# A written-out order of a cross-attention kernel's operations is replaced by another one

## The chip, the cores and the metric

The kernel runs on one core of a Trainium2 chip. The core has five instruction streams that run side by side and wait for one another by semaphores: TensorE (PE, matrix products and transposes; its weight loads are shown apart as PEld), VectorE (DVE), ScalarE (ACT), GpSimd (POOL) and SyncE (SP, which here only issues transfers between the memory of the device and that of the core). The metric is the time of one execution on the device in microseconds (us); less is better. A change below 0.3% (1.7 us here) can't be told from none.

## The reference

All arrays are 32-bit floats. `x` is 2 x 2048 x 640, the context 2 x 128 x 384; there are 8 heads of 80 numbers. Shortened to what is computed (B = 2 batches, H = 640):

```python
enc, ca = ctx[:, :124], ctx[:, 124:]              # 124 tokens of text, 4 extra ones
query, keyt, valt = x @ Wq, enc @ Wk, enc @ Wv
hs = mha(query, keyt, valt)                        # 8 heads, softmax over 124 keys
ca_q1 = einsum("btc,th->bch", ca, Wq_ca)[:, indices]   # 384 rows, spread over 2048 by linspace
ca_hs1 = mha(ca_q1, x, x)                          # softmax over 2048 rows of x
ca_hs2 = mha(ca_hs1 @ Wq, ca @ Wk_ca, ca @ Wv_ca)  # softmax over 4 keys
out = (hs + ca_hs2) @ Wout + b_out + x
```

## The kernel before

**Staging.** The work falls into stretches, each taken batch by batch. The rows of `x` come in blocks of 512 (`x_load`: pieces `xi` by transfer, turned by DVE into `xt`); PE makes the queries (`pq`) of each block, and of each block a few small products (`pyz`, `yz`) that ACT, DVE and POOL make into operands `zop`, `cop` and `y_sb` of the extra attention. The function `adapter(b)` does the extra attention of one batch. Its first half multiplies `zop` and `cop` into score tiles `s` of four PSUM banks each ("quads", 24 a batch); DVE reduces each quad to its maxima (`mx`). There is room for one quad: `quad` is `Room(1)`, and the step of DVE that reads a quad frees it. Its second half makes 24 more quads a batch, of which ACT makes exponentials (`ea`) and PE sums (`acc`). At a batch's end the sums go through ACT (`accs`), a transpose on PE (`pt_acc`) and then through `second(b)`: DVE divides (`r`, `prod`), reduces (`s2f`, `m`, `p`), ACT takes an exponential of `p`, DVE sums and turns it (`r`, `p2t`), and PE multiplies it with `rows` into `pt_p`, whose result goes out by a transfer and comes back as part of the probabilities of the text attention.

The text attention works on 16 units of 256 rows (`text(m)`): scores `sc` from the keys (`kmain`, `krest`) and the queries (`text_scores`), a softmax on DVE, ACT and DVE or POOL (`m`, `p`, `r`, the multiplication `p<-p,r`), a transposition `eb` on DVE with a round trip through the device's memory (`kept`, `pT`), the hidden rows `ph`, and the output products `po` with the parts of `Wout`. In seven units (`BY_SUMS`) the products are made with fewer rows by sums of operands (`text_out_fast`: `wout_sums`, `hs`); in the others with a high part, a low part and a mixed part of `Wout` and of the hidden rows (`text_out`: `wout_top`, `wout_low`, `wout_mix`, `ks`). DVE adds each `po` to the rows of `x` with the bias (`x_more`, `last_rows`), and SP stores the rows (`stored`). The parts `wout_low` and `wout_mix` are made after the last `acc` of batch 1, in the room of `y_sb`.

**What sets the order.** Each function is a task: a generator that yields steps `Do(engine, fn, after, needs, frees, marks, grows)`. `after` names what must have been issued before, `needs` takes places in rooms, `frees` gives them back, `marks` makes names known. The class `Desk` holds a table `ORDER` of 2366 entries; an entry is a task's number, with a letter where the engine is chosen (`a` ACT, `v` DVE, `g` POOL, `n` none). `Desk.run` walks the table, and every entry issues the next step of its task:

```python
for entry in self.ORDER.split():
    task = self.tasks[int(entry.rstrip("avgn"))]
    op = task.op
    self.engine = self.SIDES.get(entry[-1], op.engines[0])
```

Each instruction is pinned to that place, so the table sets the order of each engine's stream, of SP's transfers too. All engines run their streams in order; nothing moves at run time. L221 and L229 are the helpers of all products and transposes, L225 that of the warming products `unread`, L236 that of all work on DVE, ACT and POOL, L246 that of all transfers.

Of the kernel before, what the change touches and what calls it, by code (L numbers as in the profile page):

```python
# [8 lines left out]
F32 = mybir.dt.float32  # L9
# [5 lines left out]
P = 128  # L15
# [52 lines left out]
class Desk:  # L68
# [7 lines left out]
    2 4 4 0 2 36 0 0 2 0 0 2 0 0 2 0 0 2 0 0 2 2 124 2 4 2 0 128a 0 2 0 6 6 6 2 125 4 6 130a 126 4 131a 127 4 4  # L76
    132a 6 133v 2 3 4 6 3a 2 15 3 6 3a 15 15 3 6 3v 3 7 7 8 8 7 8 11 7 7 15 0 8 135a 0 134a 7 5 8 7 7 15 9 7
    137a 6 1 138a 136v 14 8 12 15 7 7 7 139a 7 7 141v 140v 7 142a 9 15 143a 8 144 15 9 8 8 36 8 145 5 15 15 8 8
    9 10 8 9 5 146 5 9 147 15 14 36 15 15 148 6 9 9 9 14 14 14 14 9 14 9 14g 129 152a 151v 149a 12 150v 15 153 6
    6 9 36 14 129 15 14 36 16 14g 11 9 129 129 101 36 155 155 12 155 155 11a 36 157 11 9 12 9 156a 9 155 12 158  # L80
    158 159v 158 158 158 9 36 160 162v 18 12 36 163a 12 13 36 117 123 158 17 154 158 158 158 154 154 39 161 123
    17 117v 161 165g 154 161 117v 171 175 17 161 166g 161 164 18 164 164 17 18 117g 36 164 117g 154 154 164 117g
    164 161 18 176a 164 36 164g 161 16 36 18 18 167g 171 177 16 164 16 16 16 18 36 178a 117v 117 18 43 16 36 16g
    171 181 161 117g 18 18 180 164 168g 180 36 182a 16 17 180 117g 179 180 36 179 16 171 183 16g 174 185 184a 18
    180 18 180 18 36 172 186 36 174 18 17 17 179 18 179 174 188 170 187 187 19 20 21 161 21 187 187 172 192 187
    20 189 190 21 187 36 43 36 179 179 21 173 203 203 203 191 191 36 193 191 173 204 169 103 203 191 180 36 180g
    203 191 19 21 203 21 194g 180 36 19 200 209 20 21 195g 19 36 19 191 21 39 102 210a 191 19 21 21 36 19 191
# [162 lines left out]
def kernel(  # L250
# [2116 lines left out]
```

## Time and profile before

| | us |
|---|---|
| time, median of 3 runs (lowest to highest) | 564.38 (563.48 to 564.88) |
| span of the profiled execution, first to last instruction | 562.1 |
| PE busy | 549.2 (98%) |
| DVE busy | 402.2 (72%) |
| ACT busy | 276.3 (49%) |
| POOL busy | 208.1 (37%) |
| mean granted clock of TensorE | 0.997 |

A time of the profiled execution by the clock of the runs is not recorded; the three times lie 1.4 to 2.8 us above its span, the median 2.3. The busy times are means over the whole span. In the stretch of the first quads of batch 0 (45.9 to 158.9 us) DVE is busy 105.16 of 113.0 us, in that of batch 1 (251.5 to 343.6 us) 87.97 of 92.1.

### The profile page before, as it was taken

What the parts mean: (1) busy time and instruction counts of PE and PEld (TensorE: products, weight loads), DVE (VectorE), ACT (ScalarE), POOL (GpSimd) and SP (SyncE); (2) the same over time, 40 slices, a digit from 0 to 9 for tenths busy, and PEclk for the clock granted to TensorE, in tenths of its full rate; (3) what the DMA queues carried; (4) which work ended last, traced back from release to release, by engine and by line L of the source; (5) the groups of instructions that cost most, each with busy time, mean ns of one, the idle gap of its engine ahead of it and who ended that gap; (6) DMA issues with size and microseconds to landing.
All of it is one profiled execution on the core that took longest, in us unless ns stands there. A gap on an engine that the chain in (4) does not pass through costs nothing.

```text
span 562.1 us, 17332 instructions
## 1 busy us (share of the span) xinstructions
PE 549.2 (98%) x7338; PEld 337.8 (60%) x7338; DVE 402.2 (72%) x621; ACT 276.3 (49%) x752; POOL 208.1 (37%) x206
## 2 busy tenths in 40 slices
PE   9999999999999999999999999999999899999997
PEld 8563455556555655455365445455554477989796
DVE  2457999999996564589999998655735886449542
ACT  3122645445338898886524524589878432111200
POOL 7002625344424522013559364512424830441040
PEclk9999999999999999999999999999999989999999
DMA  8994759774876899446558895859865367977533
GB/s 258 244 175 121 163 123 166 163 159 142 170 199 155 183 251 180 136 160 176 177 126 247 226 232 133 255 149 254 244 172 177 74 124 215 264 215 195 160 123 129
DMA packets 151549, 101.38 MB, mean 180 GB/s; under 512 B 86476, under 2 KB 130012, under 8 KB 151472
## 3 DMA queue, kind: packets, MB, share of 16 engines
q1 hardware_dynamic: 150704, 99.88, 69.5%
q8 instruction: 58, 0.95, 0.8%
q0 software_dynamic: 768, 0.40, 0.4%
q14 instruction: 19, 0.16, 0.1%
HBM read 61.34 MB, written 38.90 MB: 178 GB/s over the span
## 4 chain that ended last, share of the span: by engine, by line
PE 82%; DVE 7%; DMA 5%; ACT 2%; issue 2%; SPq 1%; DVEq 0%; ACTq 0%
PE po L221 23%; PE pq L221 23%; PE acc L221 7%; PE sc L221 6%; PE s L221 6%; PE ph L221 5%; PE pq_first L221 3%; PE pyz L221 3%; DVE mx L236 2%; ACT p L236 1%; DMA bias<-in_L_xattn_b_out_dram 1%; PE pk L221 1%; PE unread L225 1%; ACT ea L236 1%; PE pv L221 1%
## 5 line engine op out<-in xcount | busy, mean ns | idle before, releaser
L236 DVE TENSOR_REDUCE mx<-s 128x4 f32<-128x2048 f32 x48 | 109.2, 2275 | 2.9 <-PE s L221 2.8
L236 POOL TENSOR_TENSOR p<-p,r 128x992 f32<-128x992 f32 x29 | 53.8, 1856 | 141.1 <-DVE r L236 135.0
L236 ACT ACTIVATE ea<-s 128x2048 f32<-128x2048 f32 x48 | 90.4, 1884 | 25.6 <-PE s L221 25.3
L236 ACT ACTIVATE p<-sc,m 128x124 f32<-128x124 f32 x256 | 89.5, 374 | 25.7 <-DVE m L236 25.7
L236 ACT ACTIVATION_READ_ACCUMULATOR p<-sc,m 128x1 f32 x256 | 55.5, 217 | 0.0
L221 PE MATMUL pq<-xt,wq_sb 128*32 128x256 f32 x896 | 54.3, 381 | 0.6 <-DVE q L236 0.6
L236 DVE TENSOR_REDUCE m<-sc 128x4 f32<-128x496 f32 x64 | 40.6, 662 | 13.9 <-PE sc L221 13.7
L221 PE MATMUL acc<-ea,y_sb 128*32 128x384 f32 (+2 forms) x768 | 50.1, 383 | 0.0
L221 PE MATMUL ph<-pT,vpad 128*32 128x256 f32 x768 | 45.8, 380 | 0.8 <-DMA out_dram<-x_more 0.3
L236 DVE STREAM_TRANSPOSE eb<-p 128x1024 f32<-128x1024 f32 x32 | 39.5, 1233 | 4.5 <-POOL p L236 3.3
L221 PEld LDWEIGHTS pq<-xt,wq_sb 128*32 128x32 f32 x896 | 27.5, 110 | 22.9 <-issue 5.5
L221 PEld LDWEIGHTS sc<-kmain,q 64*128 64x128 f32 x512 | 31.8, 187 | 11.6 <-issue 8.4
L221 PE MATMUL pq<-xt,wq 128*32 128x512 f32 x320 | 38.8, 595 | 0.0
L221 PE MATMUL po<-wout_sums,hs 128*32 128x320 f32 x448 | 35.4, 438 | 3.5 <-DVE x_more L236 2.9
L221 PE MATMUL sc<-kmain,q 64*128 64x124 f32 x512 | 37.5, 283 | 0.1
L221 PE MATMUL po<-wout_sb,hs 128*32 128x320 f32 (+1 forms) x452 | 36.4, 434 | 0.7 <-DVE prod L236 0.6
L221 PE MATMUL po<-wout_low,ks 128*128 128x320 f32 x204 | 35.7, 308 | 0.0
L221 PEld LDWEIGHTS ph<-pT,vpad 128*32 128x32 f32 x768 | 24.4, 110 | 18.6 <-issue 2.6
L236 POOL TENSOR_TENSOR last_rows<-last_rows,bias 128x640 f32<-128x640 f32 x10 | 17.0, 1697 | 44.7 <-DMA last_rows<-in_x_dram 44.7
L221 PE MATMUL po<-wout_top,ks 128*128 128x320 f32 x180 | 32.5, 311 | 0.0
L221 PEld LDWEIGHTS acc<-ea,y_sb 128*32 128x32 f32 x768 | 21.1, 109 | 17.3 <-issue 8.6
L221 PEld LDWEIGHTS po<-wout_low,ks 128*128 128x128 f32 x204 | 31.3, 188 | 0.0
(232 smaller groups left out, 951.4 us busy)
## 6 DMA issues: line engine op xcount, KB each, us to landing
kept<-eb SPq DMA_DIRECT2D x32, 512.0 KB
pT<-kept SPq DMA_DIRECT2D x48, 256.0 KB
landing<-away SPq DMA_DIRECT2D x60, 128.0 KB
xi<-in_x_dram SPq DMA_DIRECT2D x28, 256.0 KB
x_more<-in_x_dram SPq DMA_DIRECT2D x17, 320.0 KB
out_dram<-x_more SPq DMA_DIRECT2D x16, 320.0 KB
last_rows<-in_x_dram SPq DMA_DIRECT2D x15, 320.0 KB
out_dram<-last_rows SPq DMA_DIRECT2D x14, 320.0 KB
```

The source lines that it names most:

```text
L221: self.pin(self.nc.tensor.matmul(out[strip], lhsT[:, strip], rhs, **kw))
L225: self.pin(self.nc.tensor.matmul(out, zeros, zeros, start=True, stop=True))
L236: return lambda *args, **kw: self.pin(getattr(engine, what)(*args, **kw))
```

## The change

The table `ORDER` is another one, of the same tasks and steps; a first and a last line of it show that it can only be read by what it does to the streams. The engine letters of some steps differ too: eight multiplications `p<-p,r` are on DVE instead of three, and eighteen additions of the bias instead of eleven. The rest of the change is small: rooms grow and come free through the steps' own lists (`grows`, `frees`) instead of inside functions, the step of the mixed part of the hidden rows is split off as `raw` and `mixing`, and a store is a task of its own in `text(m)` that waits by name for the additions to its rows instead of being started by the last of them.

```diff
     ORDER = """
-    2 4 4 0 2 36 0 0 2 0 0 2 0 0 2 0 0 2 0 0 2 2 124 2 4 2 0 128a 0 2 0 6 6 6 2 125 4 6 130a 126 4 131a 127 4 4
...
+    132 618 120 634 641 635 635 89 641 132 637 637 639 130 639 131 636 88 636 90
     """
...
-                op = yield Do("PE", scores, [("cop", b)], needs=[(quad, 1), (eas, 1)])
+                st = pieces(v)[-1][0]
+                ends_ = j == 1 and 512 * (v + 1) == CAD * (st + 1) and st % 4 == 3
+                op = yield Do(
+                    "PE", scores, [("cop", b)], needs=[(quad, 1), (eas, 1)],
+                    frees=(lambda st=st: [(zops, room_of["zop", b, st // 4])]) if ends_ else (),
+                )
...
             op = yield Do(
                 "PE", product, [("q", n), "keys", ("rest", m, k)], needs=[(banks, 2), (es, 1)], marks=[("sc", m, k)],
-            )
-            rests.give(rest_of[m, k][1])
+                frees=lambda k=k: [(rests, rest_of[m, k][1])],
+            )
...
-                op = yield Do("DVE", add, [op.at], frees=[(banks, s)] if end else [])
+                op = yield Do(
+                    "DVE", add, [op.at], frees=[(banks, s)] if end else [], marks=[("added", m, i, n, k)],
+                )
                 at = [op.at]
-                key = (m, i, 2)
-                ends.setdefault(key, []).append(op.at)
-                if len(ends[key]) == 4:
-                    yield Fork(stored(*key, ends[key]))
...
+            if m in BY_SUMS:
+                parts = (((0, 0), (0, 2), (2, 0), (3, 0)), ((0, 1), (0, 3), (1, 0), (1, 1)))[k]
+                added = [("added", m, k, *part) for part in parts]
+            else:
+                added = [("added", m, k, v) for v in ((0, 1) if u == 2 else (u,))]
+            yield Do(
+                "SP", store, added,
+                frees=lambda: [(rows, xr_of[m][k][1])] if u == 2 else [],
+            )
```

What this makes of the streams is shown at three places. In the changed kernel the helpers' lines are five smaller (L216, L224, L220, L231, L241).

The first is SP's stream near the start, where it loads the weights `w_kca`, `w_k`, `w_vca` and `w_v` and the nine pieces `xi_1` of the second block of `x`. Before:

```order
L246 DMA w_kca<-in_L_xattn_Wk_ca_dram 128x3x640
L246 DMA w_k<-in_L_xattn_Wk_dram 128x3x640
L246 DMA xi_1_268<-in_x_dram 32x64x32
L246 DMA xi_1_268<-in_x_dram 32x16x16 x2
L246 DMA w_vca<-in_L_xattn_Wv_ca_dram 128x3x640
L246 DMA xi_1_268<-in_x_dram 32x64x32
L246 DMA xi_1_268<-in_x_dram 32x16x32
L246 DMA w_v<-in_L_xattn_Wv_dram 128x3x640
```

After:

```order
L241 DMA w_kca<-in_L_xattn_Wk_ca_dram 128x3x640
L241 DMA xi_1_260<-in_x_dram 32x64x32
L241 DMA xi_1_260<-in_x_dram 32x16x16 x2
L241 DMA xi_1_260<-in_x_dram 32x64x32
L241 DMA xi_1_260<-in_x_dram 32x16x32
L241 DMA xi_1_260<-in_x_dram 32x64x32
L241 DMA xi_1_260<-in_x_dram 32x16x32
L241 DMA xi_1_260<-in_x_dram 32x64x32
L241 DMA xi_1_260<-in_x_dram 32x16x32
L241 DMA w_k<-in_L_xattn_Wk_dram 128x3x640
L241 DMA w_vca<-in_L_xattn_Wv_ca_dram 128x3x640
L241 DMA w_v<-in_L_xattn_Wv_dram 128x3x640
```

All nine pieces now stand ahead of `w_k`; before, `w_k` stood ahead of them and four more followed `w_v`. On DVE the copies `k<-w_k` now stand behind the five transpositions of these pieces and ahead of the copy `a<-pa` that feeds PE's transposes `pt_a`; before, `k<-w_k` and `a<-pa` stood ahead of those transpositions.

The second place is DVE's stream between the third and the fourth quad of batch 0. Before:

```order
L236 TENSOR_REDUCE mx_461<-s_0_0_1_0_683 128x4
L236 STREAM_TRANSPOSE yt_0_0_727<-yz_0_509 128x512
L236 STREAM_TRANSPOSE yt_0_1_732<-yz_0_509 128x512
L236 TENSOR_TENSOR wq_sums<-wq_sb 128x256 x2
L236 TENSOR_REDUCE m_0_0_752<-sc_0_0_734 128x4
L236 TENSOR_REDUCE m_0_1_753<-sc_0_1_735 128x4
L236 TENSOR_REDUCE mx_461<-s_0_0_1_1_719 128x4
```

After:

```order
L231 TENSOR_REDUCE mx_506<-s_0_0_1_0_718 128x4
L231 TENSOR_TENSOR wq_sums<-wq_sb 128x256
L231 TENSOR_REDUCE m_0_0_753<-sc_0_0_735 128x4
L231 STREAM_TRANSPOSE yt_0_0_784<-yz_0_539 128x512
L231 STREAM_TRANSPOSE yt_0_1_790<-yz_0_539 128x512
L231 STREAM_TRANSPOSE xt_2_730<-xi_2_415 128x512
L231 TENSOR_REDUCE m_0_1_754<-sc_0_1_736 128x4
L231 COPY q_757<-pq_0_758 128x2x256
L231 STREAM_TRANSPOSE xt_2_730<-xi_2_415 128x512
L231 TENSOR_REDUCE mx_506<-s_0_0_1_1_797 128x4
```

The transpositions of the third block of `x` and a copy of queries have come in between.

The third place is the end of batch 1's extra attention. On DVE before, from the last two `wout_low` to `p2t`; two more `wout_low`, `prod` and `r<-pt_acc` stand right ahead of the first row:

```order
L236 TENSOR_TENSOR wout_low<-wout_sb,wout_top_5690 128x640
L236 TENSOR_TENSOR wout_low<-wout_sb,wout_top_5692 128x640
L236 TENSOR_TENSOR wout_mix_5827<-wout_top_5694,wout_low 128x640
L236 TENSOR_TENSOR wout_mix_5828<-wout_top_5735,wout_low 128x640
L236 TENSOR_REDUCE s2f<-prod 128x8x3 x3
L236 TENSOR_REDUCE m_1_5837<-s2f 128x24
L236 TENSOR_TENSOR p_1_5732<-s2f,m_1_5837 128x96
L236 TENSOR_TENSOR x_more<-x_more,po_1_5840 128x320
L236 TENSOR_TENSOR wout_mix_5826<-wout_top_5692,wout_low 128x640
L236 TENSOR_REDUCE r_1_5734<-p_1_5732 128x24
L236 RECIPROCAL r_1_5734<-r_1_5734 128x24
L236 TENSOR_TENSOR p2t_5733<-p_1_5732,r_1_5734 128x3x8x4
```

After, from the second `wout_low` to `p2t`; another `wout_low` and two `wout_top` stand right ahead of the first row:

```order
L231 TENSOR_TENSOR wout_low<-wout_sb,wout_top_5743 128x640
L231 RECIPROCAL r_1_1_5796<-pt_acc_1_5792 128x12
L231 TENSOR_TENSOR prod<-pt_acc_1_5792,r_1_1_5796 128x3x96
L231 TENSOR_TENSOR wout_low<-wout_sb,wout_top_5759 128x640
L231 TENSOR_TENSOR wout_low<-wout_sb,wout_top_5758 128x640
L231 TENSOR_REDUCE s2f<-prod 128x8x3 x3
L231 TENSOR_REDUCE m_1_5841<-s2f 128x24
L231 TENSOR_TENSOR p_1_5736<-s2f,m_1_5841 128x96
L231 TENSOR_TENSOR last_rows<-last_rows,po_0_5718 128x320
L231 TENSOR_REDUCE r_1_5738<-p_1_5736 128x24
L231 RECIPROCAL r_1_5738<-r_1_5738 128x24
L231 TENSOR_TENSOR p2t_5737<-p_1_5736,r_1_5738 128x3x8x4
```

Two `wout_low` have moved ahead of `r<-pt_acc`, and the three `wout_mix` have moved behind `p2t`. On PE at the same place before, from the product that follows the scores of unit 15 to `pt_p`; `pt_acc` and those scores (eight products with `kmain`, eight with `krest`) stand ahead:

```order
L221 MATMUL po_1_5840<-wout_sums,hs_4309 32x320 x8
L221 MATMUL ph_0_5865<-pT_4532,vpad_107 32x256 x8
L221 MATMUL po_2_5879<-wout_sb,hs_4309 32x320 x8
L221 MATMUL po_2_5879<-wout_sb,wout_sums 32x320 x4
L221 MATMUL ph_2_5892<-pT_4532,vpad_107 32x256 x8
L221 MATMUL po_0_5703<-wout_sums,hs_4309 32x320 x8
L221 MATMUL ph_4_5915<-pT_4532,vpad_107 32x256 x8
L221 MATMUL po_1_5840<-wout_sums,hs_4309 32x320 x8
L221 MATMUL po_1_5840<-wout_sb,wout_sums 32x320 x4
L221 MATMUL pt_p_1_5950<-rows_5772,p2t_5733 32x512
```

After, from `pt_acc` on, with the scores of unit 15 ahead of it:

```order
L224 MATMUL pt_acc_1_5792<-ident,accs_1_5762 128x128 x3
L216 MATMUL po_0_5718<-wout_sums,hs_4318 128x320 x2
L216 MATMUL ph_0_5826<-pT_5370,vpad_107 32x256 x8
L216 MATMUL po_1_5856<-wout_sums,hs_4318 32x320 x8
L216 MATMUL ph_2_5865<-pT_5370,vpad_107 32x256 x8
L216 MATMUL po_3_5875<-wout_sb,hs_4318 32x320 x8
L216 MATMUL po_3_5875<-wout_sb,wout_sums 32x320 x4
L216 MATMUL po_0_5718<-wout_sums,hs_4318 32x320 x8
L216 MATMUL pt_p_1_5899<-rows_5757,p2t_5737 32x512
```

The scores of unit 15 have moved ahead of `pt_acc`, and fewer products stand between it and `pt_p`.

Elsewhere, the fourteen products `unread` all stand at the head of PE's stream (before: nine, three behind the first `pt_x`, two later), and after `pt_acc` of the first half of batch 1's sums PE has a quad and eight strips of `acc` before the first `po` (before: one `po` of three products and a quad). The table's entries between 240 and 350 us of the profile before have nearly the same order in both.

More of the change, by code (lines that the diff above doesn't have):

```diff
@@ L1587, in adapter @@
                 if j == 1 and 512 * (v + 1) == CAD * (st + 1) and st % 4 == 3:
-                    zops.give(room_of["zop", b, st // 4])
+                    late["ps_"]=0
         yield Fork(second(b))
@@ L1711, in more @@
                 late["ps"] = ctx.enter_context(tc.tile_pool(name="ps_r", bufs=1, space=bass.MemoryType.PSUM))
-                banks.grow(4)
-            yield Do("NONE", more, [])
+            yield Do("NONE", more, [], grows=[(banks, 4)])
         def product(s):
@@ L2225, in text_out, with raw, mixing, first @@
         )
+    def raw(t):
+        return t.bitcast(F32)
+    def mixing(mix, top, low, after, marks):
+        def first():
+            if desk.engine == "ACT":
+                desk.a_activation(mix(), raw(low()), AF.Identity, scale=UP)
+            else:
+                mixed(mix(), raw(top()), raw(low()))
+        op = yield Do(("DVE", "ACT"), first, after)
+        def second():
+            if op.ran == "ACT":
+                minus(mix(), raw(top()), raw(mix()))
+        yield Do(("NONE", "POOL", "DVE"), second, marks=marks)
     def hidden_parts(m, c0, n, hs, ph, s, at):
@@ L2237, in hidden_parts @@
         )
-        def scaled():
-            if desk.engine == "ACT":
-                desk.a_activation(cols("mix"), cols("low", True), AF.Identity, scale=UP)
-            else:
-                mixed(cols("mix"), cols("top", True), cols("low", True))
-        op = yield Do(("DVE", "ACT"), scaled)
-        both = op.ran == "ACT"
-        yield Do(
-            ADDS if both else "NONE", lambda: both and minus(cols("mix"), cols("top", True), cols("mix", True)),
-            marks=[("hs mix", m, c0)],
-        )
+        yield from mixing(lambda: cols("mix"), lambda: cols("top"), lambda: cols("low"), [("hs low", m, c0)], [("hs mix", m, c0)])
     def out_part(m, i, u, hs):
@@ L2275, in add, with stored, store @@
             desk.v_scalar_tensor_tensor(t, po[:, :HALF], 1.0 + DOWN, t, ALU.mult, ALU.add)
[L2277 to L2283 removed]
+        yield Do("DVE", add, [op.at, ("xr", m, i)], frees=[(banks, s)], marks=[("added", m, i, u)])
     spans = (0, HALF), (HALF, H), (0, H)
[L2286 removed]
+    def stored(m, k):
         b, st = tiles(m)[k]
[L2289 to L2294 removed]
+        for u in (2,) if m < UNITS - 1 else (0, 1):
+            def store(u=u):
+                cols = slice(*spans[u])
+                dma(out[b, st * P : (st + 1) * P, cols], xr_of[m][k][0][:, cols])
+            if m in BY_SUMS:
+                parts = (((0, 0), (0, 2), (2, 0), (3, 0)), ((0, 1), (0, 3), (1, 0), (1, 1)))[k]
+                added = [("added", m, k, *part) for part in parts]
+            else:
+                added = [("added", m, k, v) for v in ((0, 1) if u == 2 else (u,))]
[3 more added lines that the diff above has]
+            )
     blocks = [(b, sb) for b in range(B) for sb in range(NSB)]
@@ L2304, in text @@
         yield Fork(probabilities(m))
+        for k in range(2):
+            yield Fork(stored(m, k))
     begin = desk.begin
```

183 lines of the change are left out of this document (80 added, 103 removed).

## The prediction

> **What bounds the kernel now.** I read the page first, then PE's waits, then the stretches, then the timeline at each place where PE waited.
>
> ```profile
> span 562.1 us, 17332 instructions
> PE 549.2 (98%) x7338; PEld 337.8 (60%) x7338; DVE 402.2 (72%) x621; ACT 276.3 (49%) x752; POOL 208.1 (37%) x206
> ```
>
> PE is busy 549.2 of 562.1 us, and both orders give it the same products. A new order can win no more than PE's 12.9 idle microseconds and what a lower clock costs, but it can lose any amount. PE's waits say where most of it is:
>
> ```profile
> PE po L221 <- DVE x_more L236: 2.9, 1, 2.9
> PE unread L225 <- DVE zeros L236: 1.1, 1, 1.1
> PE s L221 <- DVE mx L236: 1.1, 2, 0.8
> ```
>
> (in all, times, longest.) DVE is behind the largest. The stretches (length, then busy time of PE, PEld, DVE, ACT, POOL, then the granted clock) show how near DVE is to being the bound:
>
> ```profile
> 45.90:158.90 113.00, 112.14 (x1684) 59.61 (x1680) 105.16 (x129) 52.54 (x202) 47.56 (x38) 1.00 0.70 156
> 158.90:251.50 92.60, 92.53 (x1435) 50.90 (x1431) 58.16 (x100) 75.55 (x180) 26.18 (x23) 1.00 0.75 178
> 251.50:343.60 92.10, 89.77 (x1275) 46.52 (x1274) 87.97 (x97) 43.07 (x149) 52.05 (x44) 1.00 0.73 194
> 450.60:454.00 3.40, 2.91 (x25) 1.18 (x20) 3.30 (x7) 0.95 (x3) 3.32 (x2) 0.50 0.73 153
> ```
>
> In the first quads of batch 0 (first row) DVE is busy 93% and PE idles 0.9 us; in those of batch 1 (third) DVE is at 95.5% and PE idles 2.3. The fourth row is 3.4 us at half clock, right behind the longest wait; with PE busy 2.91 of it, it costs at most 1.5.
>
> The sum is made against the span, 562.1; the median of the runs lies 2.3 above it, and I take the same 2.3 for the changed kernel.
>
> **The start, PE.** All fourteen `unread` now stand ahead of the first transpose.
>
> ```profile
> 1.11 4.21 PE L225 MATMUL unread<-zeros 128*128 128x128 f32 x18 [1.11 <-DVE zeros L236]
> 7.06 0.60 PE L229 MATMUL pt_x<-ident,xz 128*128 128x128 f32 x4
> 7.50 0.72 PE L221 MATMUL pq_first<-xt,wq_sb 128*128 128x128 f32 x5
> 7.70 0.58 ACT L236 COPY xt<-pt_x 128x512 f32<-128x512 f32 x1 [0.90 <-PE pt_x L229]
> ```
>
> Nine products are 18 instructions of 0.234 us, so fourteen end at 1.11 + 28 x 0.234 = 7.7; `pt_x` at 0.44 to 0.6 ends at 8.2; ACT's copy takes 0.58 and a short wait, so that `pq_first` starts near 8.9. Before, other transposes covered that copy; now PE waits 0.7 us. Bounds 0 to 1.4 (a second copy in the open). **+0.7.**
>
> **The start, SP and DVE.** `w_k` is issued behind nine `xi`, and DVE's copy of it now stands ahead of `a<-pa`, for which PE's `pt_a` waits.
>
> ```profile
> 10.42 0.39 SPq L246 DMA_DIRECT2D w_kca<-in_L_xattn_Wk_ca_dram  x1
> 13.65 7.72 SPq L246 DMA_DIRECT2D xi<-in_x_dram  x3
> 23.26 4.29 SPq L246 DMA_DIRECT2D xi<-in_x_dram  x2
> 28.43 8.02 SPq L246 DMA_DIRECT2D xi<-in_x_dram  x4
> 17.61 0.88 DVE L236 COPY wq<-wq_sb 128x320 f32<-128x320 f32 x2 [0.17 <-DMA w_kca<-in_L_xattn_Wk_ca_dram]
> 61.74 11.87 SPq L246 DMA_DIRECT2D xi<-in_x_dram  x9
> 32.88 0.66 PE L229 MATMUL pt_a<-ident,a 128*128 128x128 f32 x4
> ```
>
> Nine pieces took SP 20.0 us among the weights (rows two to four) and 11.9 later on (row six). From 10.9 on, `w_k` is issued between 22.8 and 30.9; a load of that size took 17.6 - 10.4 = 7.2 to land, so it is there between 30 and 38, in the middle 34. PE has 1.5 us more products ahead of `pt_a` than before and the 0.7 of above, so it wants `pt_a` at 32.9 + 2.2 = 35.1, and DVE needs about 1 us for both copies: `w_k` has to be there by 34. The middle just holds. Bounds 0 to +4; **0**, and the upper end is a rival.
>
> **The first quads of batch 0.** Counted on DVE's stream between the first and the last reduction there, the new order adds one `p` multiplication, one `eb`, one `x_sums`, one `q` addition and one `zop` addition, and lacks three copies `vpad`, one addition of `first_rests` and two of `wq_sums`.
>
> ```profile
> L236 DVE TENSOR_REDUCE mx<-s 128x4 f32<-128x2048 f32 x48 | 109.2, 2275 | 2.9 <-PE s L221 2.8
> L236 DVE STREAM_TRANSPOSE eb<-p 128x1024 f32<-128x1024 f32 x32 | 39.5, 1233 | 4.5 <-POOL p L236 3.3 <-DMA kept<-eb 1.1
> L236 DVE TENSOR_TENSOR p<-p,r 128x992 f32<-128x992 f32 x3 | 3.5, 1180 | 0.0
> L236 DVE TENSOR_TENSOR x_sums<-xt 128x512 f32<-128x512 f32 x2 | 2.5, 1246 | 0.0
> L236 DVE TENSOR_TENSOR q<-q,pq 128x512 f32<-128x512 f32 x28 | 18.6, 672 | 4.6 <-PE pq L221 4.5
> ```
>
> That is 1.23 + 1.18 + 1.25 + 0.67 + 0.67 = 5.0 more (the `zop` addition taken like that of `q`, which has its shape) and, as an estimate, 2.0 less (six rows of half that shape or smaller): +3.0, DVE 105.2 to 108.2. The first quad comes later in PE's stream, so PE's own products between first and last quad fall from about 112.7 to 109.3, and DVE goes from 93% to 99% of them. I added, quad by quad, DVE's rows between two reductions against PE's between two quads, PE waiting where its next quad would start before the last reduction has ended. For the old order that gives waits of 1.0 us (measured: 0.9) in batch 0 and 4.2 (2.3) in batch 1; for the new one 2.3 and 2.8. So **+1.3** here, bounds 0 (DVE hides as well as before) and +4.0 (below), and for **the first quads of batch 1**, where DVE has a multiplication and an `x_sums` less, **-1.3**, bounds -2.3 (no wait left) and 0.
>
> **Behind `pt_acc`, first half of batch 1.**
>
> ```profile
> 402.42 0.55 PE L229 MATMUL pt_acc<-ident,accs 128*128 128x128 f32 x3
> 402.95 1.95 DVE L236 TENSOR_TENSOR last_rows<-last_rows,bias 128x640 f32<-128x640 f32 x1
> 405.68 1.28 PE L221 MATMUL po<-wout_sb,hs 128*32 128x320 f32 x16 [0.63 <-DVE prod L236]
> ```
>
> `po` waits 0.63 for `prod`, which an addition of the bias of 1.95 us held up. Now eight strips of `acc` (about 0.9 us) stand ahead of `po`: **-0.6**, and 0 if something else holds up `prod`.
>
> **The end of batch 1's extra attention.** The costliest place; rows in order of time.
>
> ```profile
> 438.43 0.55 PE L229 MATMUL pt_acc<-ident,accs 128*128 128x128 f32 x3
> 438.91 1.16 PE L221 MATMUL sc<-kmain,q 64*128 64x124 f32 x16
> 439.02 0.23 DVE L236 RECIPROCAL r<-pt_acc 128x12 f32<-128x12 f32 x1
> 439.66 5.51 DVE L236 TENSOR_TENSOR wout_low<-wout_sb,wout_top 128x640 fp32r<-128x640 f32 x4
> 440.40 1.28 PE L221 MATMUL po<-wout_sums,hs 128*32 128x320 f32 x16
> 445.10 2.10 DVE L236 TENSOR_TENSOR wout_mix<-wout_top,wout_low 128x640 fp32r<-128x640 f32 x2
> 447.13 1.66 DVE L236 TENSOR_REDUCE s2f<-prod 128x24 f32<-128x192 f32 x3
> 449.29 0.47 DVE L236 TENSOR_TENSOR x_more<-x_more,po 128x320 f32<-128x320 f32 x1
> 449.82 1.66 PE L221 MATMUL po<-wout_sums,hs 128*32 128x320 f32 x16 [2.85 <-DVE x_more L236]
> 450.68 0.24 DVE L236 TENSOR_REDUCE r<-p 128x24 f32<-128x96 f32 x1
> 451.30 1.07 DVE L236 TENSOR_TENSOR p2t<-p,r 128x96 f32<-128x96 f32 x1
> 453.04 1.52 PE L221 MATMUL pt_p<-rows,p2t 128*32 128x512 f32 x12 [0.49 <-DVE ks L236]
> ```
>
> From `pt_acc` to `pt_p` it is 14.6 us (438.43 to 453.04), of which the waits of 2.85 and 0.49 and the half clock of at most 1.5 make some 4.8; PE has products for the other 9.8. In the new order the chain behind `pt_acc` is: 0.6 to `r` (438.43 to 439.02), 0.64 to the next row, two `wout_low` 2.75 (half of 5.51), 2.16 for `s2f`, `m` and `p` (447.13 to 449.29), 0.47 for the addition, 0.62 from the sum `r` to `p2t`, 1.07 for it: 8.3 us, since the `wout_mix` of 2.10 and a third behind it have left and two `wout_low` stand ahead. PE's products meanwhile fall too, since the scores have gone ahead: 0.48 for `pt_acc` (438.43 to 438.91), and a list nearly like that from 440.40 to the start of the wait at 446.97 (449.82 - 2.85), 6.6 us, together 7.1. That leaves a wait of 1.2 if `r` isn't late. It will be: two `wout_low` (2.75) start at the earliest when the last `acc` ends, 1.5 us of scores (438.91 to 440.40) before `pt_acc`, so `r`, ready 0.6 behind `pt_acc`, is 0.65 late at least, and 3.1 if the two `wout_top` ahead have to wait as well. So PE waits 1.9 to 4.3; I take the middle, 3.1, with the same half clock behind it: 4.6 against 4.8. **-0.2**, bounds -3.6 (1.2 and a full clock) and +1.0.
>
> **Edits at nothing.** Seven more bias additions (about 1 us each) and four more multiplications on DVE fall into stretches such as 158.90 to 251.50, where DVE is busy 58 of 93 us; uncovered they would cost up to 12 us, but PE would have to wait for each. The stores' tasks issue the same transfers; a store waits for the same additions as before, and at the end the last product, addition and store follow each other as before. The moved frees and `mixing` issue no instruction. The round trips by transfer have about as much time as before (`pt_p` to its first `ph`: 10.8 us of products against 11.0).
>
> **Sum.** 562.1 + 0.7 + 0 + 1.3 - 1.3 - 0.6 - 0.2 = 562.0 us, with 2.3 around it **564.3**: no change that can be told.
>
> **The clock.** The half clock came behind a wait of 2.85 us and lasted 3.4 (the row of 450.60 to 454.00). The Trainium skill, "TensorE: Matmul & The Clock Gate", Part 1, states that an activity window of about 3.4 us runs freely and that an idle window halves the clock; its section on oscillation asks for no idle gaps above about 3.4 us. Its length agrees with the trace; its bound does not, since 2.85 was enough here. By it a wait of 3.1, cut in two by one `po`, would leave the clock full, and the sum would be 562.8; this is part of the faster rival.
>
> **Rivals.**
>
> *Faster: the end closes up.* If DVE has the two `wout_top` behind it in time, `r` is hardly late, PE waits 1.2 instead of 3.34, no stretch is long enough to lower the clock, and the term is -3.6 instead of -0.2: 564.3 - 3.4 = 560.9. The full clock alone gives 562.8, at the edge. For it: the three `wout_mix` have left the chain. Against: the `wout_low` ahead of `r` can't start before `acc` ends.
>
> *Slower: DVE becomes the bound in the first quads of batch 0.* Where DVE had the most to do (251.5 to 343.6) it reached 95.5% and no more. If it reaches no more here, 108.2 us of work take 108.2 / 0.955 = 113.3, 4.0 above PE's 109.3, in place of +1.3: 567.0. It makes the kernel slower by over 0.3% from 3.1 us of waits in this stretch on. For it: DVE at 99% leaves nothing for an operand that is late. Against: many of the rows it took on are not in the chain of the quads.
>
> *Slower: `w_k` late.* At 38 us it costs 4.0: 568.3; above 0.3% from 35.8 on.
>
> *Nothing happens.* With PE at 98% in both, each wait that goes is replaced by one of like size; this is the forecast.
>
> **Chances.** Forecast 0.39 (own range 562.7 to 566.1); the end closing up, with gains of that kind elsewhere, 0.33; DVE the bound 0.17; `w_k` late 0.11. So faster 0.33, same 0.39, slower 0.28. The range reaches to both cases: low is the faster rival less a little (560.5), high lies between the two slower ones (568.0). The bound of 0.3% is 1.7 us, about what the runs can tell.
>
> **What would show it.** PE's idle time at the head: a wait of 0.7 for ACT's `xt`. A wait of `pt_a` for `a` near 35 us, if `w_k` is late. In the first quads of batch 0 waits of `s` for `mx` of about 2.3 us in all, in batch 1 fewer than before. No wait of `po` for `prod`. At the end a wait of `po` or `pt_p` for DVE of 2 to 4 us and a stretch of half clock behind it. The prediction is wrong if PE's waits outside these places sum to more than 2 us, above all waits for a transfer, which I have not found.

## The result, and the profile after

The changed kernel takes 573.09 us (median of four runs, 569.71 to 574.32), the kernel before, in runs beside it, 564.63 (563.48 to 566.18). The ratio is 1.0132, with an interval of 1.0092 to 1.0172: it is slower, by some 7.5 us. The profiled execution is one at the upper end, 574.32 us with a span of 572.6, so between the two traces there are 10.5 us to explain.

The page of the changed kernel, its span and the busy times:

```profile
span 572.6 us, 17365 instructions
PE 552.8 (97%) x7356; PEld 338.1 (59%) x7356; DVE 410.3 (72%) x628; ACT 281.4 (49%) x761; POOL 186.6 (33%) x196
```

PE's waits (in all, times, longest), the largest:

```profile
PE s L216 <- DVE mx L231: 3.2, 5, 1.0
PE po L216 <- DVE last_rows L231: 3.2, 4, 1.3
PE ph L216 <- DMA pT<-p: 2.6, 1, 2.6
```

One wait of 2.85 us has become many of about 1 us, and one of 2.6 for a transfer. The stretches (length, then busy time of PE, PEld, DVE, ACT, POOL, granted clock, share of the DMA engines, GB/s):

```profile
52.40:109.40 57.00, 55.99 (x786) 27.24 (x786) 55.08 (x68) 26.47 (x97) 27.70 (x25) 1.00 0.77 169
109.40:164.00 54.60, 54.60 (x869) 32.22 (x869) 51.71 (x59) 27.30 (x115) 17.65 (x13) 1.00 0.74 167
254.90:349.70 94.80, 90.12 (x1303) 45.97 (x1307) 88.15 (x97) 42.58 (x147) 52.87 (x45) 1.00 0.72 190
480.00:485.40 5.40, 4.05 (x26) 3.52 (x25) 3.02 (x6) 0.00 (x0) 1.55 (x1) 1.00 0.99 206
485.40:487.30 1.90, 0.00 (x0) 0.00 (x0) 1.90 (x5) 0.14 (x1) 0.00 (x0) 1.00 1.03 262
487.30:490.70 3.40, 2.74 (x28) 1.56 (x32) 0.86 (x3) 0.48 (x1) 1.27 (x1) 0.50 1.00 232
```

In the first quads of batch 0 (first two rows) PE idles 1.0 us, as before; in those of batch 1 (third) 4.7, against 2.3. The last three rows are new: in 10.7 us near the end PE idles 3.9, and in the last 3.4 of them the clock is at 0.50 with PE busy 2.74, which costs up to 1.4 more. There the DMA engines are full.

**Where the 10.5 us are.** PE's recorded waits sum to less than the loss, since part of it counts as busy: 552.8 us against 549.2 for the same products. (The changed kernel has 7356 records of them instead of 7338, as some are split into four narrow ones in one order and not in the other.) So I took at each quad its start, less the time of all products that PE has ahead of it, with one price for each kind of product in both orders. An example: the first quad starts at 45.26 before and 51.85 after, with 5.2 us more products ahead of it, so it is 1.4 behind. The places, in us behind the old order:

| place | behind | gained there |
|---|---|---|
| first quad of batch 0 | 1.4 | +1.4 |
| last quad of its first half (158 us before) | 2.7 | +1.35 |
| first quad of its second half (178 us after) | 3.7 | +1.0 |
| start of batch 1's quads (255 us) | 3.5 | -0.2 |
| end of batch 1's first half (350 us) | 5.8 | +2.2 |
| end of its second half (439 us) | 6.5 | +0.75 |
| `pt_p` | 4.3 | -2.2 |
| end | 10.4 | +6.1 |

I call this the ladder below. What stands behind its largest rungs is seen in the order of time. At the head, `xt` and the two products that wait for it:

```profile
7.32 0.59 ACT L231 COPY xt<-pt_x 128x512 f32<-128x512 f32 x1 [5.23 <-PE pt_x L224]
7.96 1.16 PE L216 MATMUL pq_first<-xt,wq_sb 128*128 128x128 f32 x8 [0.67 <-ACT xt L231]
...
10.23 0.94 PE L216 MATMUL pq_first<-xt,wq_sb 128*128 128x128 f32 x6 [0.24 <-ACT xt L231]
```

In batch 1's quads, DVE and PE:

```profile
307.42 0.01 DVE L231 LOAD_MASK_SELECT zs<-yz  x1 [0.77 <-DMA z<-zs]
308.09 2.28 DVE L231 TENSOR_REDUCE mx<-s 128x4 f32<-128x2048 f32 x1
310.51 0.50 PE L216 MATMUL s<-zop,cop 32*128 32x512 f32 x4 [1.04 <-DVE mx L231]
330.33 1.25 DVE L231 STREAM_TRANSPOSE eb<-p 128x1024 f32<-128x1024 f32 x1 [0.94 <-DMA kept<-eb]
331.50 2.25 DVE L231 TENSOR_REDUCE mx<-s 128x4 f32<-128x2048 f32 x1
333.90 0.51 PE L216 MATMUL s<-zop,cop 32*128 32x512 f32 x4 [0.92 <-DVE mx L231]
```

DVE waits 0.77 and 0.94 us until a store has read `zs` or `eb` (the operand is made again in the same place), the reduction behind it is late, and PE, with one place for a quad, waits 1.04 and 0.92. The same happens at 162.85, ahead of the rung of +1.0. DVE's waits of this kind in all, after:

```profile
DVE eb L231 <- DMA kept<-eb: 5.5, 6, 1.4
```

and before:

```profile
DVE eb L236 <- DMA kept<-eb: 1.1, 2, 0.8
```

At the end of the extra attention:

```profile
443.95 0.55 PE L224 MATMUL pt_acc<-ident,accs 128*128 128x128 f32 x3
445.38 0.22 DVE L231 RECIPROCAL r<-pt_acc 128x12 f32<-128x12 f32 x1
...
451.89 1.28 PE L216 MATMUL po<-wout_sums,hs 128*32 128x320 f32 x16 [1.07 <-DVE last_rows L231]
453.19 1.08 PE L216 MATMUL pt_p<-rows,p2t 128*32 128x512 f32 x12
```

`r` starts 1.4 us behind the start of `pt_acc`, 0.8 later than before, and PE's waits of 1.07 (and 0.62 at 446.19) in place of 2.85 and 0.49 left the clock at 1.00. Then, behind `pt_p`, SP's stream and what waited for it:

```profile
462.98 0.42 SPq L241 DMA_DIRECT2D pT<-kept  x1
468.32 0.52 SPq L241 DMA_DIRECT2D kept<-eb  x1
468.89 2.10 SPq L241 DMA_DIRECT2D pT<-kept  x3
471.03 0.90 SPq L241 DMA_DIRECT2D last_rows<-in_x_dram  x2
472.04 5.31 SPq L241 DMA_DIRECT2D pT<-kept  x5
478.24 1.26 SPq L241 DMA_DIRECT2D pT<-p  x2
480.80 1.55 POOL L231 TENSOR_TENSOR last_rows<-last_rows,bias 128x640 f32<-128x640 f32 x1 [4.91 <-DMA last_rows<-in_x_dram]
482.93 1.00 PE L216 MATMUL po<-wout_top,ks 128*128 128x320 f32 x5 [1.34 <-DVE last_rows L231]
487.96 4.35 PE L216 MATMUL ph<-pT,vpad 128*32 128x256 f32 x52 [2.58 <-DMA pT<-p]
```

SP issues nothing between 463.4 and 468.32: the store of `eb` stands next in its stream and waits. Then it and what stands behind it go out in one burst, eleven pieces of 224 to 512 KB in 9 us. The two loads `last_rows` in their midst are there 9.8 us after their issue (471.03 to 480.80), and the small `pT<-p` at the end of the burst 9.7 after theirs (478.24 to 487.96). PE waits for both, 1.34 and 2.58, and pays up to 1.4 for the clock: 5.3 of the rung's 6.1. SP's own wait for the step of DVE that makes this `eb` is among its waits between 455 and 490 us:

```profile
SPq L241 <- DVE eb L231: 4.8, 1, 4.8
```

### The profile page after: what moved, and what is told of

Same layout as the page of the kernel before. It is cut to its first block, busy times and chain, and to the rows that moved or that the text cites. A ratio compares the mean times of both kernels' runs of the same rounds, so it can differ in the third digit from the quotient of the medians.

```text
span 572.6 us, 17365 instructions
## 1 busy us (share of the span) xinstructions
PE 552.8 (97%) x7356; PEld 338.1 (59%) x7356; DVE 410.3 (72%) x628; ACT 281.4 (49%) x761; POOL 186.6 (33%) x196
## 4 chain that ended last, share of the span: by engine, by line
PE 63%; DVE 20%; DMA 9%; issue 3%; ACT 2%; SPq 2%; POOL 0%; DVEq 0%; ACTq 0%
PE pq L216 17%; PE po L216 17%; PE acc L216 7%; DVE mx L231 5%; PE sc L216 5%; PE s L216 5%; PE ph L216 3%; PE pq_first L216 3%; PE pyz L216 2%; DMA kept<-eb 2%; SPq L241 2%; DMA z<-zs 2%; DMA pT<-p 2%; DVE x_more L231 2%; DVE eb L231 1%
## 5 line engine op out<-in xcount | busy, mean ns | idle before, releaser
L231 ACT ACTIVATE p<-sc,m 128x124 f32<-128x124 f32 x256 | 90.0, 374 | 58.8 <-DVE m L231 58.8
L231 DVE TENSOR_REDUCE mx<-s 128x4 f32<-128x2048 f32 x48 | 109.2, 2276 | 7.0 <-PE s L216 6.9
L231 ACT ACTIVATE ea<-s 128x2048 f32<-128x2048 f32 x48 | 90.5, 1885 | 28.1 <-PE s L216 28.1
L231 POOL TENSOR_TENSOR p<-p,r 128x992 f32<-128x992 f32 x24 | 45.4, 1891 | 117.7 <-DVE r L231 107.6
L231 ACT ACTIVATION_READ_ACCUMULATOR p<-sc,m 128x1 f32 x256 | 55.4, 216 | 0.0
L216 PE MATMUL pq<-xt,wq_sb 128*32 128x256 f32 x896 | 54.7, 381 | 0.1
L231 DVE TENSOR_REDUCE m<-sc 128x4 f32<-128x496 f32 x64 | 40.9, 663 | 14.5 <-PE sc L216 14.5
L216 PE MATMUL ph<-pT,vpad 128*32 128x256 f32 x768 | 47.4, 389 | 3.4 <-DMA pT<-p 2.6
L216 PE MATMUL acc<-ea,y_sb 128*32 128x384 f32 (+2 forms) x768 | 50.0, 383 | 0.0
L231 DVE STREAM_TRANSPOSE eb<-p 128x1024 f32<-128x1024 f32 x32 | 39.5, 1235 | 5.6 <-DMA kept<-eb 5.5
L216 PEld LDWEIGHTS pq<-xt,wq_sb 128*32 128x32 f32 x896 | 28.1, 110 | 20.6 <-issue 4.9
L216 PEld LDWEIGHTS sc<-kmain,q 64*128 64x128 f32 x512 | 31.4, 187 | 13.4 <-issue 9.4
L216 PE MATMUL pq<-xt,wq 128*32 128x512 f32 (+1 forms) x302 | 39.0, 597 | 0.0
L216 PEld LDWEIGHTS ph<-pT,vpad 128*32 128x32 f32 x768 | 24.8, 112 | 22.1 <-issue 3.3
L216 PE MATMUL sc<-kmain,q 64*128 64x124 f32 x512 | 37.4, 284 | 0.3 <-ACT p L231 0.3
L216 PE MATMUL po<-wout_sb,hs 128*32 128x320 f32 x464 | 36.5, 434 | 0.8 <-DVE x_more L231 0.8
L216 PE MATMUL po<-wout_sums,hs 128*32 128x320 f32 (+1 forms) x436 | 35.2, 435 | 1.5 <-DVE last_rows L231 1.5
L216 PE MATMUL po<-wout_low,ks 128*128 128x320 f32 x204 | 35.7, 308 | 0.0
L216 PE MATMUL po<-wout_top,ks 128*128 128x320 f32 x180 | 32.7, 311 | 2.2 <-DVE last_rows L231 1.8
L216 PEld LDWEIGHTS acc<-ea,y_sb 128*32 128x32 f32 x768 | 21.1, 109 | 19.6 <-issue 11.4
L216 PEld LDWEIGHTS po<-wout_low,ks 128*128 128x128 f32 x204 | 31.3, 188 | 0.0
L231 POOL TENSOR_TENSOR hs<-hs 128x256 f32<-128x256 f32 x19 | 14.4, 766 | 51.6 <-DVE hs L231 32.3
```

Source lines behind the costliest of these rows:

```text
L216: self.pin(self.nc.tensor.matmul(out[strip], lhsT[:, strip], rhs, **kw))
L231: return lambda *args, **kw: self.pin(getattr(engine, what)(*args, **kw))
```

## The experiments

Each ratio is to the kernel before, with its interval.

**Where it is: parts of the table.** Four kernels have the changed code; a point in the two tables was chosen where both have issued the same steps, or nearly, and the old or new rows are used up to there and the other's behind it.

```diff
 e1:  ORDER = old rows throughout
 e2:  ORDER = new rows to the last of batch 0's first quads (160 us), old rows behind
 e3:  ORDER = new rows to the last of batch 1's first quads (346 us), old rows behind
 e4:  ORDER = new rows to the end of batch 1's extra attention (437 us), old rows behind
```

> The table of before in the code of the changed kernel: the new rooms, the split step and the stores that wait by name stay, every stream has the order of before. Theory (the loss is in the order alone): ratio to before 1.000 within 0.003, 564.6 us. Rival (the other edits cost something, for instance the stores' new tasks): above 1.003, up to the 573 of the changed kernel.

> The new order up to the last quad of batch 0's first half (about 160 us), the old order behind it. By the two traces PE is 3.3 us later there than its products explain (1.3 of it before the first quad). Theory (losses add up stretch by stretch): before + 3.3, about 568 us. Rival (what is lost early is waited for later anyway, and only the end counts): before + 0 to 1.

> The new order up to the last quad of batch 1's first half (about 346 us), the old order behind it. By the traces PE is 5.9 us later there. Theory: before + 5.9, about 570.5 us. Rival: as for the run before, before + 0 to 1.

> The new order up to the last quad of batch 1 (about 437 us), the old order behind it. By the traces the new order loses 6.5 us up to there and 3.9 behind it (10.4 in the profiled executions, 8.5 between the medians). Theory: before + 6.5, about 571 us, and the waits of PE for pT<-p and for last_rows near 481 to 488 us are gone, while the waits at pt_p of the old end (about 3 us and a half clock) are back. Rival (the whole loss is in the end): before + 0 to 1.

Measured: e1 564.64 us, 0.9975 (0.995 to 1.0); e2 570.63, 1.0078 (1.0047 to 1.011); e3 571.92, 1.0087 (1.0057 to 1.0117); e4 571.06, 1.0086 (1.0059 to 1.0113). So the loss is the table's: e1's five streams are those of the kernel before, step for step, it is as fast, and PE's starts lie within 0.3 us of it up to `pt_p`. (Behind the same wait of 2.85 us its clock was at 0.50 for 6.8 us, from 448.8 to 455.6, instead of 3.4, and its profiled execution ends 0.8 later: one order doesn't cost the same in every execution.) The new rows as far as 160 us cost about 4 us (2.7 to 6.2 by the interval); the ladder gives 2.7 there, and the stretch behind the seam costs another 1.4 (e2's ladder: 2.5 at the last of those quads, 3.9 where batch 1 starts). The rest of the loss lies behind 437: with the old end e4 loses 4.9 us (0.86%), with the new one 7.5. e3 and e4 don't divide the middle well. e3 has a loss of its own behind its seam (9.4 behind in the second half of batch 1), and e4 has the old end's stall back: its longest wait of `po`, 2.9 us, is one for `last_rows`.

**The quads: DVE's waits for stores (e5), or DVE's load (e10).** e5 moves four steps that wait for a transfer behind the reduction that followed them; one of the four:

```diff
-STREAM_TRANSPOSE eb_1<-p 128x1024
 TENSOR_REDUCE mx<-s_0_3_2_1 128x4
+STREAM_TRANSPOSE eb_1<-p 128x1024
```

> The new order with four steps of DVE that stood waiting for a transfer ahead of a maximum of a quad, each put behind that step: three eb (they waited 1.37, 0.36 and 0.94 us for the store kept<-eb of the eb before) and one zs (0.77 us for z<-zs). Theory (DVE's stream stands still for transfers, and quads, and so PE, stand behind it): PE is 0.5 to 1 us nearer to its products at the first quad of batch 0's second half and 1.5 to 2 us nearer at the end of batch 1's first half; 1.0132 falls to 1.008 to 1.010. Rival (DVE has simply too much work there): the waits move to other steps, PE gains under 0.5 us, no change of the ratio.

Measured: 571.61 us, 1.0118 (1.0073 to 1.0163), not told apart from the changed kernel by its time. By its ladder 2.1 us are lost instead of 3.2 between the last quads of the two batches' first halves. The wait of `s` at 310.51 is 0.25 instead of 1.04, that at 333.90 is gone, and part of that is back at the same place, since an addition now stands behind the `eb` that was moved:

```profile
333.60 1.28 PE L216 MATMUL po<-wout_sums,hs 128*32 128x320 f32 x16 [0.78 <-DVE x_more L231]
```

e10 takes work from DVE instead: the eight multiplications `p<-p,r` go to POOL.

```diff
-295v 338v 352v 361v 376v 522v 525v 562v
+295 338 352 361 376 522 525 562
```

> The new order with all eight multiplications p<-p,r that it gives to DVE on POOL, at the same places of the table; DVE has 9.4 us less to do. Theory of the prediction (DVE's load in the quads makes the loss): PE's waits for mx and x_more shrink by 1 to 3 us, ratio 1.008 to 1.011. Rival (DVE's standing waits for transfers make it, not its load): under 0.5 us, or a loss, since POOL takes 1.9 us for what DVE does in 1.2 and eb then waits for it; ratio 1.012 to 1.016.

Measured: 571.9 us, 1.0093 (1.007 to 1.0115). By its ladder batch 1's first half ends 6.5 us behind, no better than the 5.8 of the changed kernel, and its waits there have hardly moved:

```profile
PE s L216 <- DVE mx L231: 2.7, 4, 1.1
```

Less work on DVE alone mends nothing there in this trace. But it isn't a clean answer: the ratio lies where the theory put it (1.008 to 1.011), though not clear of the changed kernel's interval; the profiled execution, 573.66 us, is the slowest of six; and `eb` now waits for the slower POOL (in all, times, longest):

```profile
DVE eb L231 <- POOL p L231: 8.7, 6, 2.0
```

How much of this is the edit? In e3, e4, e6 and e9 PE and DVE have the changed kernel's order from the last quad of batch 0's first half to that of batch 1's, so the starts of the same quads can be compared without any prices. As far as the quad that starts at 329.76 in the changed kernel, that kernel takes 167.7 us and those four 167.5 to 167.9; e5 and e11 (below), which have e5's edits, both take 166.7. So three of e5's moves win about 1 us, in both kernels that have them. From there to the last quad it is 19.2 us in the changed kernel and 19.3 in e3, but 18.2 in e4, e6 and e9, with the same order. What differs is the wait at the fourth move: DVE waits 0.94 us for the store in the changed kernel and 0.56 in e3, and PE then 0.92 and 0.48; in e4, e6 and e9 the store has read `eb` in time, and neither waits. e6's step:

```profile
329.55 1.24 DVE L231 STREAM_TRANSPOSE eb<-p 128x1024 f32<-128x1024 f32 x1
```

What is shown is that DVE's waits for stores reach PE, at about 1 us for each of the two places at 310.51 and 333.90. But the second 1 us comes and goes between executions of one order, and e5's fourth move won nothing over the changed kernel's 19.2 (19.2 too, and 19.9 in e11). The rest of the 3.2 us stays open.

**The end: SP's order (e6).** The two `last_rows` loads move ahead of the store of `rows`, where SP stands still anyway, and the store of `eb` moves behind three loads of the unit before, which no longer wait behind it.

```diff
 pT<-kept 28x4x512
+last_rows<-in_x_dram 128x640 x2
 p_1<-rows 128x16x32
...
 pT<-kept 32x4x512
-kept<-eb_0 512x1x256
 pT<-kept 32x4x512 x3
-last_rows<-in_x_dram 128x640 x2
+kept<-eb_0 512x1x256
 pT<-kept 32x4x512 x3
```

> The new order with three transfers of SP moved near the end: the two loads last_rows of unit 10 from behind three pT<-kept to ahead of p<-rows, and the store kept<-eb of unit 15, on which SP stood 4.9 us, behind the three loads pT<-kept of unit 14. Theory (the end loses because transfers stand in SP's stream behind ones that wait, and then come in a burst): PE's waits of 1.34 us for last_rows and 2.58 us for pT<-p near 481 to 488 go, and with them part of the half clock: 4 to 5 us, ratio near 1.005. Rival (the transfers themselves are the bound there, the bytes come too late in any order): the wait for pT<-p stays above 2 us, and the ratio above 1.010.

Measured: 567.59 us, 1.0044 (1.0018 to 1.007), against 1.0132 for the changed kernel: about 5 us back. Its SP stream and PE:

```profile
440.05 6.76 SPq L241 DMA_DIRECT2D last_rows<-in_x_dram  x2
...
461.74 2.79 SPq L241 DMA_DIRECT2D pT<-kept  x4
467.10 0.52 SPq L241 DMA_DIRECT2D kept<-eb  x1
469.88 2.93 SPq L241 DMA_DIRECT2D pT<-kept  x5
472.85 0.65 SPq L241 DMA_DIRECT2D pT<-p  x2
...
483.17 5.39 PE L216 MATMUL ph<-pT,vpad 128*32 128x256 f32 x96
```

`pT<-p` is issued 5.4 us earlier, both waits are gone, and in the stretch that had lost most PE is busy throughout, at full clock:

```profile
480.00:500.00 20.00, 20.00 (x198) 17.51 (x197) 11.69 (x22) 4.26 (x8) 2.57 (x2) 1.00 0.95 253
```

The same row of the changed kernel:

```profile
480.00:500.00 20.00, 16.08 (x159) 12.67 (x159) 12.14 (x23) 4.26 (x8) 2.81 (x2) 0.91 1.03 235
```

No product, addition or size differs between the two. The term of the end is shown, and more than once: from `pt_p` to the end it is 113.8 to 114.0 us in the profiled executions of the three kernels that have these moves in the new rows (e6, and e8 and e11 below), and 117.1 to 119.4 in the four with the same products and the changed kernel's order of SP there (the changed kernel, e5, e9, e10). So the moves are worth 3.1 to 5.6 us by the traces. How much of it each of the two moves gives wasn't measured apart.

**The old order with a part of the new end (e7, e12).** e7 does one part of the change alone: in the old table the three `wout_mix` go behind `p2t`.

```diff
 wout_low<-wout_sb,wout_top 128x640
-wout_mix<-wout_top,wout_low 128x640 x2
 s2f<-prod 128x8x3 x3
 m_1<-s2f 128x24
 p_1<-s2f,m_1 128x96
 x_more<-x_more,po_1 128x320
-wout_mix<-wout_top,wout_low 128x640
 r_1<-p_1 128x24
 r_1<-r_1 128x24
 p2t<-p_1,r_1 128x3x8x4
 ks<-ph_0,ks 128x512
 ks<-ph_2,ks 128x512
 ks<-ks,ks 128x512
+wout_mix<-wout_top,wout_low 128x640 x3
```

> The old order (in the changed code) with one thing of the new one: the three wout_mix of DVE, and ACT's steps on them, stand behind p2t and the first sums ks. They take 3.2 us out of DVE's chain from pt_acc to pt_p. Theory (that chain alone makes the 2.85 us wait and the half clock behind it): the wait falls below 1.0 us, no half clock, 2 to 3.6 us less than before, ratio 0.994 to 0.996. Rival (POOL's rows, ready at 450.1 us, take its place): pt_p waits for POOL, about 1 us less.

Measured: 565.88 us, 1.0002 (0.9973 to 1.0031): no gain. The wait of 2.85 is 0.84, and new ones have come:

```profile
449.31 1.28 PE L216 MATMUL po<-wout_sums,hs 128*32 128x320 f32 x16 [0.84 <-DVE x_more L231]
...
455.27 0.74 PE L216 MATMUL po<-wout_sb,wout_sums 128*32 128x320 f32 x8 [1.18 <-DVE last_rows L231]
...
469.64 0.64 PE L216 MATMUL ph<-pT,vpad 128*32 128x256 f32 x8 [0.72 <-DMA pT<-p]
```

The second waits for an addition that now stands behind the `wout_mix`, the third for a round trip by transfer. `pt_p` starts 1.65 us earlier than in the kernel before (451.39 against 453.04), and the end comes 1.7 later. A gain at one place was given back at the next two.

e12 has old rows to the last quad of batch 1 and then the new end with e6's moves. If the new end, so mended, were good by itself, it would win the 2.2 us that the ladder shows at `pt_p`; the rival was that SP arrives there in another state.

```diff
 ORDER = old rows to batch 1's last quad
+        new rows behind it, with the moves of e6
```

> The old order up to the last quad of batch 1, then the new one with the three transfers of SP moved as in the run with the mended end. By the traces the new end with its mend loses 1.5 us less than the old one (span 565.9 with 5.3 lost ahead of the end, against 562.1). Theory: ratio 0.996 to 0.999, faster than both. Rival (the old stretch leaves transfers or probabilities in another state, on which the new end waits): 1.002 or more, with a wait for pT near its start.

Measured: 575.15 us, 1.0151 (1.0132 to 1.017). SP and PE:

```profile
451.17 1.73 SPq L241 DMA_DIRECT2D pT<-kept  x4
453.33 0.39 SPq L241 DMA_DIRECT2D p<-rows  x1
453.76 4.83 SPq L241 DMA_DIRECT2D pT<-kept  x2
460.10 0.25 SPq L241 DMA_DIRECT2D pT<-p  x1
464.60 1.07 PE L216 MATMUL ph<-pT,vpad 128*32 128x256 f32 x16 [3.89 <-DMA pT<-p]
```

Four loads of the unit before, which in the changed kernel were issued by 441.2 us, go out here at 451.17, right ahead of the store of `rows`; the round trip behind them is late, and PE waits 3.89 us here and 2.13 at 467.80, with the clock at 0.50 from 465.9 to 472.6. The rival is right: an end is good only for the queue that it meets.

**The head (e9, e8), and all together (e11).** e9 puts a second transpose `pt_x` and five of the `unread` between the first `pt_x` and the product that waits for its copy.

```diff
-unread<-zeros 128x128 x14
+unread<-zeros 128x128 x9
 pt_x<-ident,xz 128x128 x4
+unread<-zeros 128x128 x5
+pt_x<-ident,xz 128x128 x4
 pq_first<-xt_0,wq_sb 128x128 x4
-pt_x<-ident,xz 128x128 x4
 pt_x<-ident,xz 128x128 x4
```

> The new order with PE's head rearranged towards the old one: nine unread, the first pt_x, five unread, the second pt_x, and only then pq_first. Theory (PE waits for ACT's copies of pt_x because nothing stands between, 0.67 + 0.24 us): both waits of pq_first for xt go, the first quad comes 0.7 to 1.0 us earlier, ratio lower by 0.001 to 0.002, hardly to be told in the time but in the trace. Rival (the head then waits for something else, a load of x or of Wq): the first quad comes at the same time within 0.3 us.

Measured: 569.51 us, 1.0043 (1.0017 to 1.0069). Its waits at the head are gone, and the first quad is 0.43 us behind, not 1.4:

```profile
7.77 1.06 PE L216 MATMUL pq_first<-xt,wq_sb 128*128 128x128 f32 x8
```

The time fell by more than that 1 us. The profiled executions differ by 4.0 us; behind the head PE has the same products in the same order in both, and 0.94 of the 4.0 is there at the first quad (50.91 against 51.85), 2.24 at the last quad of batch 1's first half, 2.66 at `pt_p`. The wait for `last_rows` near the end is 0.23 instead of 1.34, while the product that waited for `pT<-p` waits as before, 2.60 (the profile now names a store, `out_dram<-x_more`). What lies behind the first quad is no larger than the differences between the other kernels with these orders (18.2 to 19.3 us at the end of batch 1's quads, 117.1 to 119.4 behind `pt_p`). So 0.94 is shown for the head, and that the early shift won the rest is not.

e8 takes the old rows up to the first quad, the new ones behind it, and the edits of e5 and e6; on SP, beside e6's, this moves `w_k`, `w_vca` and `w_v` forward again:

```diff
 w_kca<-in_L_xattn_Wk_ca_dram 128x3x640
+w_k<-in_L_xattn_Wk_dram 128x3x640
 xi_1<-in_x_dram 32x64x32
...
-w_k<-in_L_xattn_Wk_dram 128x3x640
-w_vca<-in_L_xattn_Wv_ca_dram 128x3x640
-w_v<-in_L_xattn_Wv_dram 128x3x640
```

> The new order with the old one's head (up to the first quad) and with the moves of the two runs before last together: four waiting steps of DVE behind the maxima, three transfers of SP at the end. Theory (the losses add up: 1.4 at the head, 2.5 at DVE's waits, 4 to 5 at the end): 8 us less than the new order, ratio 0.998 to 1.001. Rival (what is won at one place is lost at the next): ratio 1.005 or more.

Measured: 575.85 us, 1.0192 (1.0141 to 1.0243), a miss. Its first quad is 0.2 us ahead of the old order's, and then, at the seam:

```profile
61.98 1.02 ACT L231 CAST krest<-k_parts 128x992 fp32r<-128x992 f32 x1 [11.43 <-DMA k_parts<-k_away]
...
63.50 2.10 PE L216 MATMUL sc<-kmain,q 64*128 64x124 f32 x14 [6.04 <-ACT vpad L231]
```

The last loads of `k_parts` are issued at 57.54, behind loads of `xi` and of `first_rests` that wait for stores; in the changed kernel at 51.29. That is 6 us from SP's order alone, and the clock is at 0.50 from 61.4 to 68.2 behind it; so the run says nothing about the head by its time.

e11 has the edits of e9, e5 and e6 together, in the new table:

```diff
 ORDER = new rows
+        PE's head as in e9, DVE's four steps as in e5, SP's end as in e6
```

> The new order with all the mends: PE's head, four waiting steps of DVE behind the maxima, three transfers of SP at the end. Theory (the losses add up: about 0.9 at the head, 1.1 at DVE's waits, 5 at the end): 7 us less than the new order, ratio 1.000 to 1.003. Rival (the waits come back elsewhere): no better than the mended end alone, 1.0044.

Measured: 566.68 us, 1.0017 (1.0001 to 1.0034). Three places mended bring the changed kernel from 1.3% to 0.2% above the kernel before, as expected, and no further. By its ladder it is 2.4 us behind at the start of batch 0's second half and 4.6 at the end of batch 1's. Most of that comes at the end of batch 1's first half, where PE waits 0.78 at 332.12 for the addition behind the `eb` that was moved, and 0.81 at 343.40. No version run here is shown to be faster than the kernel before.

## Why the prediction was wrong

By its steps:

- **The step that failed is "Edits at nothing"**, its sentence on the round trips: "about as much time as before (`pt_p` to its first `ph`: 10.8 us of products against 11.0)". I measured what PE has to do meanwhile and not what SP has to do ahead. The time of a round trip is set by the queue, and by what the step in front of it waits for. That term was 0 and measured +6.1; e6 returns about 5 of it with three moves on SP. The first round trip, for which the 10.8 us stand, was in time; the late one is the next, whose loads stand behind the store of `eb`. I had found no wait for a transfer, and said that one would make the prediction wrong; SP's stream behind `pt_p` was not walked through.
- **"The first quads of batch 1"**: -1.3 forecast, +2.2 measured. The sum of DVE's rows between two reductions took every row as ready at once. DVE's waits for its own stores, 1.1 us in all before and 5.5 after (all stretches), were left out; 1 us of this is shown by e5 and e11, and another by the wait at 333.90, which some executions don't have. Nor did DVE's work there fall, as I had counted: it is 88.15 us against 87.97, with 95 steps between the first and the last reduction in both (a multiplication, a copy of `q` and an `m` less, a `zs`, an `hs` and an addition to `last_rows` more).
- **"The first quads of batch 0"**: +1.3 forecast, +1.35 measured; the rival in which DVE becomes the bound there (4.0) did not occur. The rung of +1.0 behind it, between 162 and 178 us, where an `eb` waited 1.37 for its store, was in no step.
- **"The start, PE"**: the mechanism was right, 0.67 of wait for ACT's `xt`, but a second wait of 0.24 and smaller ones came behind it: 1.4 for 0.7, the bound that was named. e9 returned 0.95 of it. **"The start, SP and DVE"**: `w_k` was not late; no wait of `pt_a` for `a`.
- **"Behind `pt_acc`, first half of batch 1"**: -0.6 forecast, -0.7 measured; no wait for `prod` is left. The rest of that half gave +1.5, unforeseen.
- **"The end of batch 1's extra attention"**: -0.2 forecast, -2.2 measured. `r` was 0.8 us late and not 1.9 or more, since the two `wout_top` were done in time, and waits of 0.62 and 1.07 did not lower the clock. That was the mechanism of the faster rival; it happened, and was outweighed nearly 3 to 1 by what followed.
- **The clock.** The Trainium skill, "TensorE: Matmul & The Clock Gate", its section on oscillation, asks for no idle gaps above about 3.4 us. The traces agree that short waits pass (1.07 after and 2.0 in e5 at full clock) and not with the bound: in an idle time of 2.58 us, with 1.34 shortly ahead of it, the clock fell to 0.50 after 1.9 us and stayed there for 3.4, as it did behind 2.85 before.

My steps summed to -0.1. The same places came to 1.4 + 1.35 + 2.2 - 0.7 - 2.2 = +2.05; what lies outside them, 1.0 - 0.2 + 1.5 + 6.1 = +8.4, is most of the error.

## What to carry to other kernels

Where a planner's table moves transfers, walk SP's stream as closely as the engines': for each transfer that someone waits for, list what stands ahead of it in the queue, what that waits for, and how many bytes go out at once behind a wait. An operation that writes where a store still reads is a wait for a transfer too; put it behind the short step on which the bound engine waits, not ahead of it, and look at what then waits behind it (e5's fourth move won nothing). A stall that goes at one place is a gain only if the next operand is ready earlier as well: e7 removed 2 us of it for nothing, and e12 lost 8 with an end that had won 2 elsewhere.

## What the runs showed of the hardware

A transfer of 32 KB at the tail of a burst of eleven larger pieces needed 9.7 us from its issue to the product that waited for it, with the DMA engines at 0.99 to 1.03 of their time; `w_kca`, nearly 1 MB, needed 7.2 at the start of the profile before. And one order doesn't lose the same in every execution: at one `eb` DVE waited 0.94, 0.56 or 0 us for the landing of a store, and PE 0.92, 0.48 or 0 behind it (the changed kernel; e3; e4, e6 and e9), and behind a wait of 2.85 us the clock was at 0.50 for 3.4 us before and for 6.8 in e1. The times scatter in the same way with either table: 563.85 to 569.83 us over 31 runs of the kernel before beside e1 to e4, 567.70 to 572.95 over ten of e2.
